# Layer 2's inputs issued behind the attention's last sum, image 2 loaded into score tiles, and scan carries copied by POOL

## The chip, the cores and the metric

The kernel runs on one core of one Trainium2 chip. The metric is device time in microseconds. The engines are PE (TensorE, matmuls), DVE (VectorE), ACT (ScalarE), POOL (GpSimd) and SP (SyncE, which here only issues DMAs); each works through its own queue in order.

## The reference

The input x is 4 images of 512 channels by 32x32 positions, in float32. Two layers follow one another, each added to its input.

```
x = x + mamba(groupnorm(x))
x = x + pab(groupnorm(x))
```

The first layer, per image: layer norm over channels, a projection to 2 x 1024 rows (xm and z), a causal convolution of 4 taps and SiLU (xs), a projection of xs to dt, B and C, and then for each of 1024 rows and 16 states a recurrence over the 1024 positions:

```
h = exp(dt*A) * h + (dt*xs) * B        # one scan for each row and state
y = sum over states of h * C
out = ((y + xs*D) * silu(z)) @ W_out
```

The second layer, per image: two 1x1 convolutions to 64 channels (top, center), their product of all positions with all positions (1024x1024 scores), a softmax over the whole map, the product of that map with a 3x3 convolution of the image, the image added, and a second 3x3 convolution.

## The kernel before, in words

**First layer.** The work is cut into stages: image b, pair of 128-row groups e (0 to 3), half h of the 1024 positions. That makes 4 x 4 x 2 = 32 stages of 16 states s each; one stage and state is a `unit`. In a unit, ACT makes the decay exp(dt*A) (L832). The input part comes in one of two ways: for nine states, ACT scales transposed rows by B (L844) and PE transposes them back (L870); for the other seven, POOL multiplies by B (L859). DVE runs two scans of 128x512 (L884), one for each 128-row group j. The product with C follows: for states 1, 5, 9 and 13 (`C_ON_DVE`) on DVE (L900, in two halves), for the other twelve on POOL (L906, one instruction of 128x1024). PE adds the result into y (L913). A stage ends when ACT copies y out (L936).

The second half of the positions goes on where the first ended. So for h = 0, DVE copies the last column of each scan to `carry_sb` right behind the scan (L889, 128x1), and the scan with h = 1 of the same state, one stage later, starts from it.

The order of all this isn't written out. Each operation is a `step` with an engine, a cost in us, its reads and writes and a priority. A planner (`Plan.issue`) runs through these costs, always takes the step that can start first or is most urgent, and so writes the order of every engine's queue. A scan costs 1.18 in it, 1.32 with the copy; the C product on POOL 2.31. Other work is laid between the units by priority: the projection and convolution of the next image, the output projection of the image before, and the transform of 3x3 weights for the second layer ("fill" steps on POOL).

**Second layer.** The 3x3 convolutions are done in a transformed domain (Winograd, 4 x 2 outputs). `conv3` takes an image, makes its transformed inputs in three pairs (for the first pair `first_inputs`: ACT L1393, POOL L1394, DVE L1396 and L1397, then `spread` L1374 to L1377; for the other pairs POOL L1456, L1457, L1466, L1467 and DVE L1460, L1469), and multiplies them with 24 weight tiles of 1 MB, loaded by SP into three buffers (L1490, L1494). DVE combines the products (L1510). Five PSUM buffers (`pm`) hold these products; three others (`ps`) serve everything else.

Per image b the order in the program is: `conv3("b")`, then `attend` (PE L1546 multiplies the score tiles with the convolution's result in 8 blocks; DVE adds each block into the image, L1559), and in between `scores` for the next image of the pair (PE L1324 makes top and center, ACT copies them to SBUF at L1329 and L1336; PE L1345 makes the scores, ACT copies them into eight `st` tiles at L1349; DVE takes maxima, L1350). During the attention of images 0 and 1, DVE also transforms the second convolution's remaining weights (`piece`, L1421 to L1432). After both images of a pair, `conv3("o")` runs for each, and `finish` adds the result to the stored input and writes it out (SP loads at L1576, PE L1586, DVE L1591, ACT stores at L1601).

`norm` makes the normalised image: ACT issues 8 loads of 256 KB (L1285) into a tile with the tag "v", which the transformed inputs use too, DVE takes statistics (L1292, L1293), PE averages over groups (L1299, L1303), ACT makes the root, DVE writes the image (L1306). For image 2 this happens inside `conv3("o1")`, through `mid`. Here the framework's scheduler sets the order on each engine, from the program's order and its own view of what is ready; tiles of one tag take turns in that tag's buffers, and an instruction waits for the buffer's last users.

Of the kernel before, what the change touches and what calls it, by code (L numbers as in the profile page):

```python
# [8 lines left out]
F32 = mybir.dt.float32  # L9
# [6 lines left out]
P = 128  # L16
B, C, HH, WW = 4, 512, 32, 32
L = HH * WW
NCC = C // P
# [4 lines left out]
T = 512  # L24
# [145 lines left out]
def mamba_then_pab_kernel(  # L170
# [25 lines left out]
    nc = tc.nc  # L196
# [23 lines left out]
    brow = []  # L220
# [46 lines left out]
    image = {}  # L267
# [6 lines left out]
    with ExitStack() as l0:  # L274
# [539 lines left out]
        def unit(b, e, h, s, y):  # L814
# [49 lines left out]
            for j, u in enumerate(us):  # L864
                part = parts[j]
                if on_act:

                    def turn(j=j, u=u):
                        for k in range(NK):
                            nc.tensor.transpose(  # L870
                                u()[:, k * P : (k + 1) * P], sc()[:, k, j, :], ident
                            )

                    step(
                        "ACT", EXP, lambda j=j: decay(j, hc()[:, j]), [dt], [part], prio, "exp",
                        holds=[hc],
                    )
                    step("PE", 4 * TR, turn, [sc], [u], prio - PRM["kt"])
                else:
                    step("ACT", EXP, lambda j=j, u=u: decay(j, u()), [dt], [u], prio - PRM["ke"], "exp")  # L880

                def scan(j=j, u=u):
                    ht = u() if on_dve else hc()[:, j]
                    nc.vector.tensor_tensor_scan(  # L884
                        ht, *((hc()[:, j], u()) if on_act else (u(), hc()[:, j])),
                        carry_sb[:, j, s : s + 1] if h else 0.0, ALU.mult, ALU.add,
                    )
                    if h == 0:
                        nc.vector.tensor_copy(carry_sb[:, j, s : s + 1], ht[:, T - 1 : T])  # L889

                before, behind = ([carry[s][j]], []) if h else ([], [carry[s][j]])
                step(
                    "DVE", SCAN if h else SCAN + 0.14, scan,
                    [part if on_act else hc, u, *before],
                    [u if on_dve else part, *behind], prio - 1, holds=[hc],
                )
                if on_dve:
                    step(
                        "DVE", 0.6,
                        lambda j=j, u=u: nc.vector.tensor_mul(hc()[:, j], u(), c_bc()[:, 0]),  # L900
                        [u, c_bc], [part], prio, holds=[hc],
                    )
            if not on_dve:
                step(
                    "POOL", 2.31,
                    lambda: nc.gpsimd.tensor_mul(hc(), hc(), c_bc().to_broadcast([P, 2, T])),  # L906
                    [c_bc], parts, prio, holds=[hc],
                )
            for j in range(2):

# [349 lines left out]
    with ExitStack() as l1:  # L1260
# [15 lines left out]
        NMC = L // P  # L1276
        HR = T // WW

        def norm(b):

            xg = padded(b, *((cpool, "image"), (gp, "xg"))[b % 2])
            t = xp.tile([P, NCC, L], F32, tag="v", name=f"x1t_{b}")
            for c in range(NCC):
                for h in range(NH):
                    nc.scalar.dma_start(  # L1285
                        t[:, c, h * T : (h + 1) * T], x1[b][h][c * P : (c + 1) * P, :]
                    )
            mv = spool.tile([P, NCC, 2], F32, tag="mv", name=f"mv_l1_{b}")
            for c in range(NCC):
                bs = spool.tile([P, NH, 6], F32, tag="bs", name=f"bs_l1_{b}_{c}")  # L1290
                for h in range(NH):
                    nc.vector.bn_stats(bs[:, h, :], t[:, c, h * T : (h + 1) * T])  # L1292
                nc.vector.bn_aggr(mv[:, c, :], bs)  # L1293
            mean, rstd, dev = (
                spool.tile([P, NCC], F32, tag=n, name=f"{n}_l1_{b}")
                for n in ("gmean", "grstd", "gdev")
            )
            p1 = ps.tile([P, T], F32, tag="ps", name=f"pm_l1_{b}")
            nc.tensor.matmul(p1[:, :NCC], gm_sb, mv[:, :, 0], start=True, stop=True)  # L1299
# [5 lines left out]
            for c in range(NCC):  # L1305
                nc.vector.tensor_scalar(  # L1306
                    xg[:, c, 1 : HH + 1, 1 : WW + 1],
                    t[:, c].rearrange("p (h w) -> p h w", w=WW),
                    mean[:, c : c + 1], rstd[:, c : c + 1], ALU.subtract, ALU.mult,
                )  # L1310
            image[b] = xg

        def scores(b, xg):

# [121 lines left out]
            for q in (1, 2):  # L1436
                nc.sync.dma_start(dst[q], o[:, q - 1])

        def conv3(name, xg, u, bias, first=None, late=None, mid=None):

# [34 lines left out]
            y = [None] * 4  # L1475
            for pair in PAIRS:
                if pair == (1, 2):
                    v = first or first_inputs(name, xg)
                    if mid:
                        mid()  # L1480
                else:
                    v = spread(name, pair[0], inputs(pair))
                ns = []
# [53 lines left out]
        def attend(b, xg, st, rp, xb, between, also):  # L1537

            ahead = piece_taps(also[0]) if also else None


            for k in range(NCC * NH):
                j, h = divmod(k, NH)
                pt = ps.tile([P, C], F32, tag="ps", name=f"pat_{b}_{j}_{h}")
                for m in range(NMC):
                    nc.tensor.matmul(  # L1546
                        pt, st[m][:, 2 * P * j + h : 2 * P * (j + 1) : 2],
                        xb[m // 2][:, m % 2, :],
                        start=(m == 0), stop=(m == NMC - 1),
                    )  # L1550
# [8 lines left out]
                nc.vector.scalar_tensor_tensor(  # L1559
                    img, pt.rearrange("p (h w) -> p h w", w=WW), rz, img,  # L1560
                    ALU.mult, ALU.add,
                )
                if also:
                    taps = piece_taps(also[k + 1]) if k + 1 < len(also) else None
                    piece(*ahead)
                    ahead = taps
                    if taps is None:
                        also = []

        dst = [out[b].rearrange("(c p) h w -> p c (h w)", p=P) for b in range(B)]  # L1570

# [44 lines left out]
        def normed(b):  # L1616
            for _ in norm(b):
                pass

        left = list(range(EARLY, NPC))  # L1620
        half = len(left) // 2
        st, rp = scores(0, image[0])
        for a in range(0, B, 2):
            for b in (a, a + 1):
                xb = conv3(f"b{b}", image[b], ub, brow[0])
                also = left[b * half : (b + 1) * half] if not a else []
                after, v = iter(()), None
                if b == a:
                    after = norm(b + 1)
                    next(after)  # L1630
                else:
                    v = first_inputs(f"o{a}", image[a])
                attend(b, image[b], st, rp, xb, after, also)
                if b == a:
                    st, rp = scores(b + 1, image[b + 1])
            finish(a, conv3(f"o{a}", image[a], uo, brow[1], v))
            if a + 2 == B:
                last(a + 1, image[a + 1], None)
                break
            y = conv3(f"o{a + 1}", image[a + 1], uo, brow[1], mid=lambda: normed(a + 2))  # L1640
            finish(a + 1, y)
            st, rp = scores(a + 2, image[a + 2])


# [55 lines left out]
```

## Time and profile before

| | us |
|---|---|
| runs: median of 3 | 3060.0 |
| runs: lowest and highest | 3053.99, 3060.22 |
| the profiled execution's own time | 3048.93 |
| its span in the profile | 3047.1 |

| engine | busy us | share of the span |
|---|---|---|
| PE | 2742.4 | 90% |
| DVE | 2402.3 | 79% |
| POOL | 2022.1 | 66% |
| ACT | 1842.4 | 60% |

The two layers differ: from 187 to 1992 us (31 of the 32 stages) DVE is busy for 1689.9 of 1805 us, PE for 1606.1, ACT for 1595.6 and POOL for 1562.9; after that PE is the busy one. In lines of the profile, a name such as `da` or `uw_b` is a tile's name without its number: `hc` of the source is `da` (states with B on ACT) or `dbx` (the others). `[5.86 <-DVE xg L1559]` says that the engine stood idle for 5.86 us before the line's first instruction, and that this wait ended with DVE's instruction of line 1559. A float32 matmul shows as two passes. A PE busy time can hold slow passes: the granted clock of a stretch tells.

### The profile page before, as it was taken

The page shows a single profiled execution, that of the slowest core. Times are in us where ns is not written, and L with a number is a line of the kernel's source. Part 1 is how long each engine was busy: PE and PEld are TensorE (multiplying, and loading weights), DVE is VectorE, ACT ScalarE, POOL GpSimd, SP SyncE. Part 2 cuts the span into 40 slices and gives each one's busy share as a digit, 9 for nine tenths or more (in the row PEclk, how much of TensorE's full clock was granted, in tenths as well). Part 3 has the DMA queues.
Part 4 walks back from the last instruction along what each step waited for, and adds up shares of the span by engine and source line. Part 5 has one row for each costly group of instructions (what it writes and reads, how often), then busy time and mean ns, then how long its engine had stood idle before and what let it go on. Part 6 is the DMA issues. An engine that isn't in the chain of part 4 may idle for free.

```text
span 3047.1 us, 35912 instructions
## 1 busy us (share of the span) xinstructions
PE 2742.4 (90%) x11512; PEld 1607.5 (53%) x11512; DVE 2402.3 (79%) x3171; ACT 1842.4 (60%) x3179; POOL 2022.1 (66%) x1047
## 2 busy tenths in 40 slices
PE   4789789999889999889999978799899999999998
PEld 2346556656666666556666655544344444444444
DVE  3469999989999989989999999976857575456164
ACT  4579989998789999789999888731110013030000
POOL 7899977899967889967889999843321331323132
PEclk8899999999999999989999999999999999999999
DMA  6766534567734567734566654748588896727497
GB/s 179 213 192 210 168 121 141 164 207 231 232 109 145 166 180 229 251 116 133 168 184 213 209 177 141 171 154 297 170 286 263 301 330 246 264 70 275 138 316 256
DMA packets 408947, 610.47 MB, mean 200 GB/s; under 512 B 46488, under 2 KB 245400, under 8 KB 384184
## 3 DMA queue, kind: packets, MB, share of 16 engines
q1 hardware_dynamic: 399952, 593.67, 61.8%
q10 hardware_dynamic: 8648, 14.26, 1.3%
q8 instruction: 92, 1.51, 0.2%
q14 instruction: 95, 0.78, 0.1%
q0 software_dynamic: 160, 0.26, 0.0%
HBM read 511.09 MB, written 96.99 MB: 200 GB/s over the span
## 4 chain that ended last, share of the span: by engine, by line
PE 45%; DVE 23%; ACT 16%; DMA 6%; issue 5%; POOL 4%; SPq 1%; ACTq 0%; DVEq 0%; POOLq 0%
PE m_o L1494 10%; PE m_b L1494 9%; DVE da L884 7%; PE y L913 5%; PE pz L394 4%; ACT sc L844 4%; PE pat L1546 4%; DVE u L884 3%; ACT da L832 3%; PE po L394 2%; PE u L870 2%; ACT u L832 2%; DVE dbx L884 2%; PE pxm L394 2%; PE psc L1345 2%
## 5 line engine op out<-in xcount | busy, mean ns | idle before, releaser
L906 POOL TENSOR_TENSOR da<-da,cbc 128x1024 f32<-128x1024 f32 x288 | 680.3, 2367 | 151.3 <-DVE carry_sb L889 63.6
L859 POOL TENSOR_TENSOR dbx<-dtx,bbc 128x1024 f32<-128x1024 f32 x224 | 529.6, 2368 | 59.1 <-PE y L913 34.9
L844 ACT ACTIVATE sc<-dtxt,bt_sb 128x256 f32<-128x256 f32 x1152 | 504.6, 497 | 46.2 <-PE u L870 46.0
L832 ACT ACTIVATE da<-dt,a_sb 128x512 f32<-128x512 f32 x576 | 395.0, 713 | 39.2 <-PE y L913 33.5
L884 DVE TENSOR_TENSOR_SCAN da<-da,carry_sb,u 128x512 f32<-128x512 f32 x288 | 356.0, 1262 | 27.3 <-PE u L870 22.0
L913 PE MATMUL y<-ident,da 128*128 128x128 f32 x2304 | 320.4, 283 | 58.3 <-POOL da L906 54.4
L870 PE MATMUL u<-ident,sc 128*128 128x128 f32 x2304 | 336.1, 278 | 35.3 <-DVE da L884 24.9
L913 PEld LDWEIGHTS y<-ident,da 128*128 128x128 f32 x2304 | 268.5, 145 | 161.2 <-POOL da L906 109.9
L884 DVE TENSOR_TENSOR_SCAN da<-da,u 128x512 f32<-128x512 f32 x288 | 348.8, 1211 | 3.9 <-PE u L870 3.6
L1494 PE MATMUL m_o<-uw_o,v_o 128*128 128x512 f32 x768 | 337.9, 599 | 4.4 <-DMA uw_o<-u_o 4.4
L1494 PE MATMUL m_b<-uw_b,v_b 128*128 128x512 f32 x768 | 333.4, 593 | 4.1 <-DMA uw_b<-u_b 4.1
L870 PEld LDWEIGHTS u<-ident,sc 128*128 128x128 f32 x2304 | 268.4, 143 | 112.2 <-DVE da L884 37.2
L832 ACT ACTIVATE u<-dt,a_sb 128x512 f32<-128x512 f32 x448 | 297.4, 681 | 36.8 <-DVE dbx L900 14.0
L394 PE MATMUL pxm<-xt,winc 128*128 128x345 f32 (+3 forms) x704 | 251.3, 499 | 29.3 <-DMA winc<-in_w_in_dram 16.5
L913 PE MATMUL y<-ident,dbx 128*128 128x128 f32 x1792 | 252.9, 279 | 23.7 <-POOL dbx L906 14.4
L913 PEld LDWEIGHTS y<-ident,dbx 128*128 128x128 f32 x1792 | 207.5, 143 | 99.7 <-issue 32.2
L394 PE MATMUL pz<-xt,winc 128*128 128x512 f32 x512 | 242.1, 600 | 11.7 <-ACT sz L707 2.1
L1494 PEld LDWEIGHTS m_o<-uw_o,v_o 128*128 128x128 f32 x768 | 145.9, 192 | 188.0 <-issue 180.7
L1494 PEld LDWEIGHTS m_b<-uw_b,v_b 128*128 128x128 f32 x768 | 145.0, 190 | 188.9 <-issue 179.5
L906 POOL TENSOR_TENSOR dbx<-dbx,cbc 128x1024 f32<-128x1024 f32 x96 | 226.7, 2362 | 26.0 <-DVE carry_sb L889 17.5
L1546 PE MATMUL pat<-y_b,st 128*128 128x512 f32 x512 | 221.6, 593 | 1.6 <-DVE rz L1555 1.5
L394 PEld LDWEIGHTS pxm<-xt,winc 128*128 128x128 f32 x704 | 132.0, 198 | 117.1 <-issue 62.1
(235 smaller groups left out, 4331.5 us busy)
## 6 DMA issues: line engine op xcount, KB each, us to landing
cbc<-bcd SPq DMA_DIRECT2D x512, 256.0 KB, 3.6
uw_b<-u_b SPq DMA_DIRECT2D x96, 1024.0 KB, 4.8
uw_o<-u_o SPq DMA_DIRECT2D x96, 1024.0 KB, 4.8
bbc<-bcd SPq DMA_DIRECT2D x224, 256.0 KB, 3.6
u_b<-work SPq DMA_DIRECT2D x192, 128.0 KB, 2.8
winc<-in_w_in_dram SPq DMA_DIRECT2D x72, 256.0 KB, 3.8
szd<-sz SPq DMA_DIRECT2D x32, 512.0 KB, 3.5
szl<-szd SPq DMA_DIRECT2D x32, 512.0 KB, 5.0
```

What stands on the lines that cost most here:

```text
L394: lambda k=k, lhs=lhs, rhs=rhs: nc.tensor.matmul(p()[:, at : at + cols], lhs(), rhs(), start=(k == 0), stop=(k == n - 1)),
L832: nc.scalar.activation(t, dt()[:, j], AF.Exp, scale=a_sb[:, at : at + 1])
L844: nc.scalar.activation(sc()[:, k], dtxt()[:, k], AF.Copy, scale=bt[:, at, s : s + 1])
L859: lambda: nc.gpsimd.tensor_mul(hc(), dtx(), b_bc().to_broadcast([P, 2, T])),
L870: nc.tensor.transpose(u()[:, k * P : (k + 1) * P], sc()[:, k, j, :], ident)
L884: nc.vector.tensor_tensor_scan(ht, *((hc()[:, j], u()) if on_act else (u(), hc()[:, j])), carry_sb[:, j, s : s + 1] if h else 0.0, ALU.mul ...
L906: lambda: nc.gpsimd.tensor_mul(hc(), hc(), c_bc().to_broadcast([P, 2, T])),
L913: nc.tensor.matmul(y[j]()[:, k, :], hc()[:, j, k * P : (k + 1) * P], ident, start=(s == 0 and k == 0), stop=(s == NS - 1 and k == NK - 1), ...
L1345: nc.tensor.matmul(pt, top[:, m * P : (m + 1) * P], center[:, h * T : (h + 1) * T], start=True, stop=True,)
L1494: nc.tensor.matmul(m[q], v[:, q, k, c, :], w[:, c, :], start=(c == 0), stop=(c == NCC - 1 and not extra),)
L1546: nc.tensor.matmul(pt, st[m][:, 2 * P * j + h : 2 * P * (j + 1) : 2], xb[m // 2][:, m % 2, :], start=(m == 0), stop=(m == NMC - 1),)
```

## The change

In the scans, for the twelve states with the C product on POOL, DVE no longer copies the carries; POOL copies both last columns of a unit (128x2) right ahead of its C product. The planner's costs follow (scan 1.18; POOL 2.5 for the two), and `carry` is now written by the POOL step. In the second layer, `attend` returns its last sum, and the inputs of the second image of a pair (`first_inputs`, all engines' instructions; the one on DVE gets the edge) are issued behind it on DVE. `norm` is cut in three parts. For image 2 its data goes into four tiles of tag "st", its loads and statistics come ahead of `conv3("o0")`, the mean behind it, and the root and the image behind `finish` of image 0.

```diff
-                    if h == 0:
+                    if h == 0 and on_dve:
                         nc.vector.tensor_copy(carry_sb[:, j, s : s + 1], ht[:, T - 1 : T])
 
-                before, behind = ([carry[s][j]], []) if h else ([], [carry[s][j]])
-                step(
-                    "DVE", SCAN if h else SCAN + 0.14, scan,
+                before, behind = ([carry[s][j]], []) if h else ([], [carry[s][j]] if on_dve else [])
+                step(
+                    "DVE", SCAN + 0.14 if h == 0 and on_dve else SCAN, scan,
...
             if not on_dve:
-                step(
-                    "POOL", 2.31,
-                    lambda: nc.gpsimd.tensor_mul(hc(), hc(), c_bc().to_broadcast([P, 2, T])),
-                    [c_bc], parts, prio, holds=[hc],
+                def times_c():
+                    if h == 0:
+                        nc.gpsimd.tensor_copy(carry_sb[:, :, s : s + 1], hc()[:, :, T - 1 : T])
+                    nc.gpsimd.tensor_mul(hc(), hc(), c_bc().to_broadcast([P, 2, T]))
+
+                step(
+                    "POOL", 2.31 if h else 2.5, times_c,
+                    [c_bc], [*parts, *([] if h else carry[s])], prio, holds=[hc],
                 )
...
-        def norm(b):
-
-            xg = padded(b, *((cpool, "image"), (gp, "xg"))[b % 2])
-            t = xp.tile([P, NCC, L], F32, tag="v", name=f"x1t_{b}")
+        def norm(b, spare=False):
+
+            if spare:
+                ts = [xp.tile([P, L], F32, tag="st", name=f"x1t_{b}_{c}", bufs=NMC) for c in range(NCC)]
+            else:
+                t = xp.tile([P, NCC, L], F32, tag="v", name=f"x1t_{b}")
+                ts = [t[:, c] for c in range(NCC)]
...
+            yield
             p1 = ps.tile([P, T], F32, tag="ps", name=f"pm_l1_{b}")
             nc.tensor.matmul(p1[:, :NCC], gm_sb, mv[:, :, 0], start=True, stop=True)
             deviation(p1, mv, mean, dev)
...
-            for c in range(NCC):
+            xg = image[b] = padded(b, *((cpool, "image"), (gp, "xg"))[b % 2])
+            for c, t in enumerate(ts):
...
-                    v = first or first_inputs(name, xg)
-                    if mid:
-                        mid()
+                    with tc.issue_after(behind.ins) if behind else ExitStack():
+                        v = first or first_inputs(name, xg)
...
-                nc.vector.scalar_tensor_tensor(
+                ins = nc.vector.scalar_tensor_tensor(
                     img, pt.rearrange("p (h w) -> p h w", w=WW), rz, img,
                     ALU.mult, ALU.add,
                 )
...
+            return ins
...
         for a in range(0, B, 2):
+            ins = None
             for b in (a, a + 1):
-                xb = conv3(f"b{b}", image[b], ub, brow[0])
+                xb = conv3(f"b{b}", image[b], ub, brow[0], behind=ins)
...
                 if b == a:
                     after = norm(b + 1)
                     next(after)
+                    next(after)
                 else:
                     v = first_inputs(f"o{a}", image[a])
-                attend(b, image[b], st, rp, xb, after, also)
+                ins = attend(b, image[b], st, rp, xb, after, also)
...
-            finish(a, conv3(f"o{a}", image[a], uo, brow[1], v))
+            if a + 2 < B:
+                after = norm(a + 2, True)
+                next(after)
+            y = conv3(f"o{a}", image[a], uo, brow[1], v)
+            next(after, None)
+            finish(a, y)
...
-            y = conv3(f"o{a + 1}", image[a + 1], uo, brow[1], mid=lambda: normed(a + 2))
-            finish(a + 1, y)
+            next(after, None)
+            finish(a + 1, conv3(f"o{a + 1}", image[a + 1], uo, brow[1]))
```

More of the change, by code (lines that the diff above doesn't have):

```diff
@@ L1277, in mamba_then_pab_kernel @@
         HR = T // WW
-        def norm(b):
-            xg = padded(b, *((cpool, "image"), (gp, "xg"))[b % 2])
-            t = xp.tile([P, NCC, L], F32, tag="v", name=f"x1t_{b}")
-            for c in range(NCC):
+        def norm(b, spare=False):
[5 more added lines that the diff above has]
+            for c, t in enumerate(ts):
                 for h in range(NH):
                     nc.scalar.dma_start(
-                        t[:, c, h * T : (h + 1) * T], x1[b][h][c * P : (c + 1) * P, :]
+                        t[:, h * T : (h + 1) * T], x1[b][h][c * P : (c + 1) * P, :]
                     )
             mv = spool.tile([P, NCC, 2], F32, tag="mv", name=f"mv_l1_{b}")
-            for c in range(NCC):
+            for c, t in enumerate(ts):
                 bs = spool.tile([P, NH, 6], F32, tag="bs", name=f"bs_l1_{b}_{c}")
                 for h in range(NH):
-                    nc.vector.bn_stats(bs[:, h, :], t[:, c, h * T : (h + 1) * T])
+                    nc.vector.bn_stats(bs[:, h, :], t[:, h * T : (h + 1) * T])
                 nc.vector.bn_aggr(mv[:, c, :], bs)
@@ L1304, in norm @@
             rsqrt(rstd, p2[:, :NCC])
-            for c in range(NCC):
+            xg = image[b] = padded(b, *((cpool, "image"), (gp, "xg"))[b % 2])
+            for c, t in enumerate(ts):
                 nc.vector.tensor_scalar(
                     xg[:, c, 1 : HH + 1, 1 : WW + 1],
-                    t[:, c].rearrange("p (h w) -> p h w", w=WW),
+                    t.rearrange("p (h w) -> p h w", w=WW),
                     mean[:, c : c + 1], rstd[:, c : c + 1], ALU.subtract, ALU.mult,
                 )
-            image[b] = xg
         def scores(b, xg):
@@ L1437, in piece, with conv3 @@
                 nc.sync.dma_start(dst[q], o[:, q - 1])
-        def conv3(name, xg, u, bias, first=None, late=None, mid=None):
+        def conv3(name, xg, u, bias, first=None, late=None, behind=None):
             def rows(a):
@@ L1614, in last @@
                 (nc.scalar, nc.sync)[j % 2].dma_start(dst[b][:, j, :], o[j])
-        def normed(b):
-            for _ in norm(b):
-                pass
         left = list(range(EARLY, NPC))
```

## The prediction

> **What bounds the kernel now.** I read the engines' busy shares by stage first, since the two parts of the change sit in different layers. Layer 1 (the scans) runs to about 1995 us, layer 2 from there to 3047. A stretch of undisturbed scan stages of the last image (columns: stretch, length, then busy us of PE, PE weight load, DVE, ACT, POOL):
>
> ```profile
> 1643.00:1944.00 301.00, 259.67 (x1527) 182.60 (x1525) 295.41 (x383) 252.16 (x465) 282.20 (x132) 0.99 0.61 178
> ```
> and all that DVE waits for in it:
> ```profile
> DVE dbx L884 <- ACT u L832: 0.9, 1, 0.9
> DVE da L884 <- PE u L870: 0.6, 1, 0.6
> DVE dbx L884 <- POOL dbx L859: 0.3, 1, 0.3
> ```
> DVE waits 1.8 of 301 us: it sets the pace here, with POOL (282) close behind. A second sign: taking a stage to end at its y copies (L936), the stages of image 3 with h = 0 (which save carries) last 50.5, 51.3, 52.5, 51.0 us, those with h = 1 50.1, 48.6, 47.9, 48.4. The cost of a carry copy, from DVE in order of time:
> ```profile
> 1000.28 1.22 DVE L884 TENSOR_TENSOR_SCAN u<-u,dbx 128x512 f32<-128x512 f32 x1
> 1001.53 0.16 DVE L889 COPY carry_sb<-u 128x1 f32<-128x1 f32 x1
> 1001.61 1.22 DVE L884 TENSOR_TENSOR_SCAN u<-u,dbx 128x512 f32<-128x512 f32 x1
> ```
> Scan to scan takes 1.33 us with a copy; without one, two scans in a row take 2.37, so 1.19 each. A copy costs DVE 0.14 us, though it is booked as 0.15.
>
> In layer 2 the chain of waits is nearly all PE, so I looked for PE's gaps. Two large ones touch the change. The first stands between image 0's attention and image 1's scores:
> ```profile
> 2170.91 3.61 PE L1324 MATMUL pt<-xg,wt_sb 128*128 128x512 f32 x8
> 2176.76 3.71 PE L1324 MATMUL pt<-xg,wt_sb 128*128 128x512 f32 x8 [2.24 <-DVE xg L1559]
> 2180.31 1.88 PE L1494 MATMUL m_b<-uw_b,v_b 128*128 128x512 f32 x4
> 2188.05 5.36 PE L1345 MATMUL psc<-center,top 128*128 128x512 f32 x6 [5.86 <-DVE xg L1559]
> 2198.03 14.08 PE L1345 MATMUL psc<-center,top 128*128 128x512 f32 x26 [4.62 <-ACT st L1349]
> ```
> DVE and ACT show why: the last two sums (L1559) stand among image 1's transform inputs, and the score copies stand behind an input of the output convolution that waits for DVE.
> ```profile
> 2175.96 0.75 DVE L1559 SCALAR_TENSOR_TENSOR xg<-pat,rz,xg 128x512 f32<-128x512 f32 x1
> 2182.55 3.55 DVE L1376 TENSOR_TENSOR v_b<-rr_b 128x1024 f32<-128x1024 f32 x1
> 2187.16 0.74 DVE L1559 SCALAR_TENSOR_TENSOR xg<-pat,rz,xg 128x512 f32<-128x512 f32 x1
> 2196.39 1.11 ACT L1393 ACTIVATE e_o<-xg 128x1088 f32<-128x1088 f32 x1 [13.94 <-DVE rr_b L1469]
> ```
> The second gap is in the output convolution of image 1, where PE's group mean for image 2 waits for statistics queued on DVE behind an output sum:
> ```profile
> 2456.59 1.41 DVE L1591 TENSOR_TENSOR o<-o,po 128x256 f32<-128x256 f32 x4 [6.66 <-DMA o<-x]
> 2460.72 0.56 PE L1299 MATMUL pm_l<-mv_l,gm_sb 128*128 128x4 f32 x2 [6.05 <-DVE mv_l L1293]
> 2461.14 5.35 PE L1494 MATMUL m_o<-uw_o,v_o 128*128 128x512 f32 x6
> ```
> And a smaller one, where image 2's loads will now go:
> ```profile
> 2353.83 8.70 PE L1494 MATMUL m_o<-uw_o,v_o 128*128 128x512 f32 x16 [3.05 <-DMA uw_o<-u_o]
> ```
>
> **What the Trainium skill says.** "TensorE: Matmul & The Clock Gate", What's actually happening: after an idle window of about 3.4 us the array falls to half clock and needs a busy window to come back. The trace agrees: granted clock 0.50 at 2188 to 2190 and at 2462 to 2466, 0.86 us a pass in place of 0.43; even the 3.05 us gap costs clock, the 2.24 us gap doesn't. "GPSIMD Engine Reference", 3.1 Elementwise: GpSimd reaches an instruction over two software hops, against DVE's dispatch of some 156 ns; no figure for a tiny copy. The trace gives a fixed part: 0.73, 1.28 and 2.37 us for 256, 512 and 1024 elements leave 0.185 us at none. The same page, 1. Specifications: GpSimd shares SBUF interfaces with DVE instructions of two SBUF inputs. Agrees: L1375 and L1376 took 3.55 us each beside POOL's L1466 and L1467, 1.22 elsewhere. "DMA: Bandwidth & Descriptors", Queues, rings and completion order: each DMA engine takes turns between queues. The trace can't show the turns, but x1t loads land in a median 7.2 us and the four times larger weights in 4.8.
>
> **Part 1, scans.** 12 of 16 states multiply by C on POOL. For h = 0 that is 4 images x 4 pairs x 12 = 192 units, and 384 DVE copies go: 384 x 0.14 = 53.8 us off DVE, 3.4 in each of the 16 stages with h = 0. Added are 192 POOL copies of 128x2. No such row exists. From below, the 128x1 memset: 0.10 us; from above, the fixed 0.185 plus a semaphore's wait, 0.25. I take 0.15 (two POOL products follow one another 0.06 closer than their length, so 0.185 is partly covered): 1.8 us a stage, 29 us in all, between 19 and 48. The y matmuls behind each product see the scan end 0.14 sooner and POOL 0.15 later: even. The h = 1 scan that reads the carry comes 16 units later, so that wait is hidden.
>
> Now who takes over. In an undisturbed stage POOL has 19 products at 2.31 us and two at 1.28: 46.4. With the copies 48.2, where the stage lasts 51.3 and DVE falls from 51 to 47.6. So POOL is next; I count 2.5 us for each of the three such stages of image 3 (7.5), and 2 for the two of images 1 and 2 (4). In the six heavy h = 0 stages, which carry the next image's projection (62 to 73 us; DVE 91 to 97% busy, POOL 63 to 92%, ACT 85 to 98%), 2 each: 12. First stages of an image are ACT's (50.9 of 51 us at 1592 to 1643): 0.5 each, 1.5; image 0's early ones 1. Sum 26. The planner's new costs move every later step; the built kernel shows 7 more ACT table loads in layer 1 at 1.28 us = 9 us, five in image 1, of which I put 4 on the path. **Layer 1: -22 us**, bounds -45 (nearly all of the 53.8) and +5 (POOL and ACT eat it).
>
> **Part 2, inputs behind the last sum.** In the built order both sums precede L1396, and the score copies precede e_o. From 2170.91 to the end of the scores PE has 16 + 4 + 32 = 52 passes at 0.43 = 22.4 us but takes until 2211.95, 41.0: 12.7 idle, 5.9 half clock. Afterwards: sums at 2173.5 and 2174.2 (L1432 ends at 2173.5), so the second pt starts at once and ends at 2177.9. The first transform group needs L1374; L1396 (free of the rr buffer at 2174.75) starts at 2174.9, L1374 ends at 2178.6, so PE waits 0.7. ACT's top copies end at 2180.0, the scores start at 2180.4 and, copied in 0.58 us each against PE's 0.86, end at 2194.1. **-17.9 us** (-12 if an input or the weights hold PE again; -18.6 at most). What is late next: DVE mixes eight maxima (1.22) with the remaining inputs and reaches L1510 near 2206.5; PE needs the accumulator that it frees at about 2215. Next weights again wait for SP's o loads, which wait for the scores: the 1.3 us gap at 2223 stays. For image 3 PE had no gap; inputs are ready at 2706.6 and PE needs them at 2709.0. Nothing, but only 2.4 us of cover.
>
> **Part 3, image 2 in score tiles.** Its 8 loads (2 MB), statistics (8 x 0.68 + 4 x 0.19 = 6.2 us of DVE) move from 2439 to about 2348, when attention frees the tiles. At 2460 the wait goes: 6.05 + (5.35 - 2.6) = 8.8 us; the two tiny matmuls remain (0.5), and the weights, which follow the o load on SP, should land just in time. **-8 us** (-5 to -8.5). The price: at 2348 PE is already waiting for the first uw_o. Sharing turns with x1t it lands some 2.5 us later, and the longer idle costs about 0.9 of clock: **+3.4 us** (0 to 6). ACT's issues hold up e_o1 and f_o1, and DVE's statistics the last sum and L1510; the next PE user of either (the sixth accumulator, near 2377) is over 10 us away. The four border memsets (1.2 us of POOL) move to where POOL idles.
>
> **Sum.** -22 - 17.9 - 8 + 3.4 = -44.5. The profiled execution took 3048.9 us (span 3047.1), so 3004.4. The runs shown have a median of 3060.0, 11.1 above; on that footing 3015.5, and I give 3016.
>
> **Rivals.** POOL takes DVE's place in layer 1 (22%): for it, 46.4 of 51 us and POOL's 13.7 us of idle in the stretch above; against, its room in heavy stages. Layer 1 gives about 2, total 3036. DVE really was the only limit (15%): for it, the 1.8 us of waits; layer 1 gives 40, total 2998. The layer 2 gap only changes its releaser (8%), for instance weights or inputs hold the scores: part 2 gives 4, total 3030. Slower (6%): the tiny POOL copy is dear. Each h = 0 stage then ends with POOL at 46.4 + 12c; layer 2's 22.5 is lost over 16 stages from 46.4 + 12c - 51.3 = 1.4, c = 0.53 us; at 0.8 us the stages lose 4.7 each, 75 in all, total 3112. Against it: the 0.185. That the edits don't act is excluded for the order (the build shows it).
>
> **Numbers.** Forecast case 45% (its own range 3006 to 3026), rivals 22, 15, 8 and 6%, and 4% for a re-planned layer 1 that gives the gain back. Within 0.2% (6 us, what can be told from no change here): 4%; slower 6%; faster 90%. The range 2994 to 3042 leaves out the slow cases and the far end of the quick ones.
>
> **What would show it.** Right: stages with h = 0 about as long as those with h = 1; POOL copies of 0.1 to 0.25 us; scores of image 1 in one run of 14 us with no idle before; no wait at L1299 for image 2; a longer wait for uw_o near 2350. Wrong: DVE idle in the stages of image 3 with POOL at 98%, copies over 0.5 us, or PE waiting for uw_b or v_b before the scores.

## The result, and the profile after

| | before | after |
|---|---|---|
| runs: median, us | 3056.99 (4 runs) | 3012.82 (4 runs) |
| runs: lowest and highest | 3049.64, 3060.22 | 3012.06, 3018.19 |
| the profiled execution's own time, its span | 3048.93, 3047.1 | 3013.52, 3011.5 |
| busy us of PE, DVE, ACT, POOL | 2742.4, 2402.3, 1842.4, 2022.1 | 2732.6, 2324.8, 1846.0, 2054.5 |

The ratio is 0.9872, with a 95% interval of 0.9851 to 0.9893: 44 us between the medians, 35.4 between the two profiled executions. The forecast was 3016.

Where the 35.6 us of span went can be read off marks that both traces have. Image 0's first scores in layer 2 start at 2014.4 before and at 2000.4 after, so 14.0 lie ahead of them, in the scans, and 21.6 behind. In layer 2 the largest single piece is image 1's score gap, from PE's first `pt` to the end of the scores: 41.0 us before (2170.91 to 2211.95), 22.3 after (2158.74 to 2181.08), so 18.7.

**Scans.** An undisturbed stretch of the last image after the change (stretch, length, then busy us of PE, PE weight load, DVE, ACT, POOL):

```profile
1630.00:1930.00 300.00, 265.41 (x1562) 188.56 (x1560) 287.44 (x314) 255.96 (x473) 289.78 (x164) 0.97 0.58 179
```

What DVE waits for in it (total, times, longest):

```profile
DVE res L1001 <- PE po L394: 7.5, 6, 4.4
DVE dbx L884 <- ACT u L832: 2.4, 3, 1.3
DVE da L884 <- PE u L870: 1.6, 2, 1.0
DVE total L1061 <- PE po L394: 1.2, 1, 1.2
...
```

DVE fell from 295.4 of 301 us to 287.4 of 300, and POOL rose from 282.2 to 289.8: POOL is now slightly the busier of the two, and DVE waits 13.9 us in all where it waited 1.8. The new instruction, in order of time on POOL:

```profile
1684.72 0.18 POOL L906 COPY carry_sb<-da 128x2 f32<-128x2 f32 x1
1684.98 2.37 POOL L907 TENSOR_TENSOR da<-da,cbc 128x1024 f32<-128x1024 f32 x1
1687.30 2.38 POOL L859 TENSOR_TENSOR dbx<-dtx,bbc 128x1024 f32<-128x1024 f32 x1
1689.62 0.19 POOL L906 COPY carry_sb<-da 128x2 f32<-128x2 f32 x1
1689.89 2.37 POOL L907 TENSOR_TENSOR da<-da,cbc 128x1024 f32<-128x1024 f32 x1
```

The copy itself is 0.18 or 0.19 us, but the product that follows starts 0.26 to 0.27 after the copy's start. From the start of one long instruction to that of the next POOL needs 2.32 us without a copy between them (1684.98 to 1687.30) and 2.59 with one (1687.30 to 1689.89). Over all such pairs without idle time the medians are 2.32 and 2.58. So a copy costs POOL 0.25 to 0.27 us.

**Layer 2, the score gap.** PE's order of time after (the bracket is idle time before, and what ended it):

```profile
2158.74 7.05 PE L1332 MATMUL pt<-xg,wt_sb 128*128 128x512 f32 x16
2165.64 1.88 PE L1501 MATMUL m_b<-uw_b,v_b 128*128 128x512 f32 x4
2167.35 13.90 PE L1353 MATMUL psc<-center,top 128*128 128x512 f32 x32
2181.08 5.31 PE L1501 MATMUL m_b<-uw_b,v_b 128*128 128x512 f32 x12
2213.23 3.27 PE L1501 MATMUL m_b<-uw_b,v_b 128*128 128x512 f32 x7 [1.55 <-ACT e_b L1509]
```

And DVE's, at the place where the sums and the inputs used to be mixed:

```profile
2159.47 1.40 DVE L1566 SCALAR_TENSOR_TENSOR xg<-pat,rz,xg 128x512 f32<-128x512 f32 x2
2160.80 1.29 DVE L1404 TENSOR_TENSOR rr_b<-e_b,f_b 128x1088 f32<-128x1088 f32 x1
```

Both sums (L1566, formerly L1559) go ahead of the first input, the two `pt` follow one another, and the scores are one run of 13.9 us. The three waits of 2.24, 5.86 and 4.62 us are gone. A new one of 1.55 us comes later.

**Layer 2, the second convolutions.** PE's first weights of image 0's output convolution, and image 2's group mean with what follows it:

```profile
2325.19 8.53 PE L1501 MATMUL m_o<-uw_o,v_o 128*128 128x512 f32 x16 [5.04 <-DMA uw_o<-u_o]
...
2410.34 0.28 PE L1307 MATMUL pm_l<-mv_l,gm_sb 128*128 128x4 f32 x2
...
2426.72 3.70 PE L1501 MATMUL m_o<-uw_o,v_o 128*128 128x512 f32 x8 [0.20 <-DMA uw_o<-u_o]
```

The 6.05 us wait of the group mean (L1299 before, L1307 now) is gone. The wait for the first `uw_o` grew from 3.05 to 5.04.

### The profile page after: what moved, and what is told of

It reads as the page before. It is cut to its first block, busy times and chain, and to the rows that moved or that the text cites. A ratio compares the mean times of both kernels' runs of the same rounds, so it can differ in the third digit from the quotient of the medians.

```text
span 3011.5 us, 35733 instructions
## 1 busy us (share of the span) xinstructions
PE 2732.6 (91%) x11512; PEld 1611.4 (54%) x11512; DVE 2324.8 (77%) x2787; ACT 1846.0 (61%) x3186; POOL 2054.5 (68%) x1239
## 4 chain that ended last, share of the span: by engine, by line
PE 39%; ACT 14%; DVE 14%; POOL 6%; issue 5%; DMA 4%; SPq 0%; DVEq 0%; POOLq 0%; ACTq 0%
PE m_o L1501 11%; PE m_b L1501 8%; PE pat L1553 4%; PE y L917 4%; ACT sc L844 3%; DVE da L884 3%; PE po L394 3%; POOL da L907 3%; PE pz L394 2%; ACT da L832 2%; ACT u L832 2%; PE u L870 2%; DVE u L884 2%; DVE dbx L884 2%; PE pp L730 1%
## 5 line engine op out<-in xcount | busy, mean ns | idle before, releaser
L859 POOL TENSOR_TENSOR dbx<-dtx,bbc 128x1024 f32<-128x1024 f32 x224 | 529.5, 2371 | 35.7 <-PE y L917 18.7
L870 PE MATMUL u<-ident,sc 128*128 128x128 f32 x2304 | 329.3, 279 | 35.1 <-DVE da L884 26.6
L884 DVE TENSOR_TENSOR_SCAN da<-da,u 128x512 f32<-128x512 f32 x288 | 338.4, 1202 | 18.6 <-PE u L870 16.7
```

The costliest lines, as they stand in the source:

```text
L859: lambda: nc.gpsimd.tensor_mul(hc(), dtx(), b_bc().to_broadcast([P, 2, T])),
L870: nc.tensor.transpose(u()[:, k * P : (k + 1) * P], sc()[:, k, j, :], ident)
L884: nc.vector.tensor_tensor_scan(ht, *((hc()[:, j], u()) if on_act else (u(), hc()[:, j])), carry_sb[:, j, s : s + 1] if h else 0.0, ALU.mul ...
```

## The experiments

Ratios are against runs of the kernel before on the same chip. For the scans I also use one length from each profile: from the first stage's first y copy to the last stage's first y copy ("scan length"). It repeats well between executions with the same scans: 1754.5, 1756.7 and 1756.0 us for the scans of before (the kernel before, e1, e5), 1738.7, 1738.2, 1739.3 and 1737.8 for those of after (after, e2, e8, e12).

**One part alone.** e1 has the scans of before with all of after's layer 2, e2 the reverse; e5 is before with the issue-behind edge alone.

```diff
 e1: carry copies and costs as before; layer 2 as after
 e2: carry copies and costs as after; layer 2 as before
 e5: before, and
+                    with tc.issue_after(behind.ins) if behind else ExitStack():
+                        v = first or first_inputs(name, xg)
```

> Only the changes of the second layer; the scans are those of before, with DVE copying the carries. My theory: from the traces of before and after, the second layer gives 21 us (18.7 at the scores of image 1, 7 at the output convolution of image 1, less 2 at the first output weights and about 3 of smaller waits elsewhere), so about 0.993 of before, 3035 us. Rival: the whole gain is the second layer's and re-ordered scans gave nothing: 0.987. Rival: the layers are not additive, since the scans' new end moves what the second layer meets: below 12 us.

> Only the changes of the scans; the second layer is that of before. My theory: the first scores of image 0 start 14 us sooner, as in the traces, and nothing follows: about 0.9955, 3043 us. Rival: layer 1 gives the 22 us that I forecast and the profiled execution of before was a fast one: 0.993.

> The kernel before with one edit: the second image's inputs of a pair are issued behind the attention's last sum. My theory: this alone closes the gap at the scores of image 1, 18 us, and pays back 2 to 3 us at two later waits for ACT's copy of an accumulator: 15 us faster, ratio 0.995. Rival: without the norm of image 2 moved, DVE and SP are late elsewhere and eat it: under 8 us.

| | median us | ratio | 95% |
|---|---|---|---|
| e1, layer 2 alone | 3033.23 | 0.9945 | 0.9933 to 0.9957 |
| e2, scans alone | 3032.61 | 0.9941 | 0.9930 to 0.9953 |
| e5, edge alone | 3037.91 | 0.9945 | 0.9928 to 0.9962 |

In us that is -17 for layer 2, -18 for the scans: together -35 of the change's -39 (1.28% of 3050). The parts add up within the intervals. The edge alone gives as much as all of layer 2, so image 2's new place nets nothing that runs can resolve. The profiles show why. From image 1's `pz` (the small matmul early in the attention that adds up the softmax's row sums) to the first bias pass of image 0's output convolution takes 60.1 us before, 61.95 after. Single profiles scatter here, so I take all that are kept: 58.2 to 60.7 us in the five with before's layer 2 or with the edge alone (before, e2, e3, e5, e10), 61.95 to 63.7 in the six with after's layer 2 (after, e1, e4, e7, e9, e11). The means differ by 3.6: that is what the early loads cost. From there to image 2's first scores takes 192.5 before, 185.5 after, 185.4 in e1: 7.0 gained.

**The moved copy without the new plan.** e3 has POOL's copies but gives the planner the costs of before, so each queue keeps its old order.

```diff
-                    "DVE", SCAN + 0.14 if h == 0 and on_dve else SCAN, scan,
+                    "DVE", SCAN + 0.14 if h == 0 else SCAN, scan,
...
-                    "POOL", 2.31 if h else 2.5, times_c,
+                    "POOL", 2.31, times_c,
 (layer 2 as before)
```

> The scans' change with the planner's costs left as before (scan 1.32 with h = 0, C product 2.31), so that every queue keeps the order of before and only the 384 copies on DVE give way to 192 on POOL. My theory: the copy costs POOL 0.27 us (0.19 and 0.08 until the product starts), POOL takes over the pace in stages without a projection, and the gain is about the same as with the new order: 10 to 16 us. Rival: the new order with its 7 more table loads cost some 8 us, then this one gains 20 to 24 us. Other rival: the gain came from the new order, then this one gains under 5 us.

Measured: 3061.29, ratio 1.0041 (1.0029 to 1.0053), 12.5 us slower than before, where my theory and both rivals had it faster. The same instructions on the same engines, in the old order, lose time. DVE's waits over 187 to 1992 us, of before and then of e3 (total, times, longest):

```profile
DVE da L884 <- PE u L870: 25.6, 20, 2.7
DVE dbx L884 <- ACT u L832: 14.1, 13, 2.9
```
```profile
DVE da L884 <- PE u L870: 42.7, 36, 3.8
DVE dbx L884 <- ACT u L832: 26.5, 25, 3.1
```

DVE has less to do, 1617 us in place of 1690, and waits more. But these waits alone don't explain the loss. In e10 (below; its line numbers are one higher), which has the same order and no copies of the twelve states at all, more than half of their rise is there too:

```profile
DVE da L885 <- PE u L871: 35.3, 28, 3.8
DVE dbx L885 <- ACT u L833: 22.3, 20, 3.1
```

And yet e10 is faster than before. What sets e3 apart from e10 is POOL's copies alone. PE's waits for POOL's C products, ahead of the y matmuls, add up to 68.8 us before, 74.4 in e10 and 91.0 in e3. That these waits rose is measured; which of them sets the pace was not separated.

**The new plan without the moved copy, and no copy at all.** e9 keeps after's queue orders but leaves the copies on DVE. e4 is after without POOL's copies, e10 has before's scan order without the copies of the twelve states and before's layer 2.

```diff
 e9 (costs of after; layer 2 as after)
-                    if h == 0 and on_dve:
+                    if h == 0:
                         nc.vector.tensor_copy(carry_sb[:, j, s : s + 1], ht[:, T - 1 : T])
...
-                    if h == 0:
-                        nc.gpsimd.tensor_copy(carry_sb[:, :, s : s + 1], hc()[:, :, T - 1 : T])
 e4 (after), e10 (order of before): no copy for these states,
+        nc.gpsimd.memset(carry_sb, 0.0)
```

> The changed kernel with the order of all queues kept, but the carries copied by DVE behind each scan, as before. Theory one: the new order helps only because it fits the new durations, so with DVE's 54 us back the scans lose all of the gain and more, 17 to 30 us above the changed kernel. Theory two: the new order is simply a better one, whichever engine copies: within 5 us of the changed kernel. Theory three: the work on DVE decides, then 10 to 15 us above it.

> The changed kernel, same order of all queues, with POOL's 192 carry copies left out: for the twelve states whose C product is POOL's, the carry stays at zero, so the second half of the positions starts from an empty state there. My theory: POOL's copies set the pace in 16 stages, 12 x 0.27 = 3.2 us a stage, and about a third to a half of these 51 us is on the path: 15 to 25 us below the changed kernel, near 2993 us. Rival: POOL's copies fall into its waits and cost nothing: same as the changed kernel within 4 us.

> The kernel before, same order of all queues, with DVE's 384 carry copies left out and none on POOL: the carry of the twelve states with POOL's C product stays at zero, so their second half starts from an empty state. Theory one: with the queues' order fixed, the 54 us that DVE gains turn into waits; under 10 us faster, ratio above 0.997, so the loss of the run with POOL copies in the old order (+12.5 us) is POOL's copies standing in the fixed order. Theory two: DVE sets the pace, 25 us or more faster, below 0.992.

| | median us | ratio | 95% |
|---|---|---|---|
| e9, new order, DVE copies | 3037.73 | 0.9950 | 0.9931 to 0.9968 |
| e4, new order, no copies | 3005.15 | 0.9852 | 0.9839 to 0.9864 |
| e10, old order, no copies | 3037.72 | 0.9950 | 0.9932 to 0.9968 |

With layer 2's -17 taken off e9 and e4, the scans alone stand as follows against before (runs), with the scan length from the profile in brackets:

| scans, us | old order | new order |
|---|---|---|
| DVE copies | 0 (1754.5) | about +2 (1759.4) |
| no copies | -15 (1741.5) | about -28 (1729.0) |
| POOL copies | +12.5 (1763.6) | -18 (1738.7) |

Each figure from runs has an interval of some 4 to 6 us either way, and the two measures agree cell by cell to a few us. With the copies made at all, the gain needs both halves: the new order with the old copies is worth nothing, the old order with the new copies loses. In the old order the POOL copies cost 22 us of scan length over no copies, in the new one 10; that is less than the 15 to 25 that I expected of e4. e9 is 24 us above after by the ratios, as its theory one had it. e10 lies between its two theories: of the 54 us taken off DVE, 15 reach the total.

**Is the order lucky, and how dear is a copy?** e11 charges the planner 2.58 for copy and product, the measured 2.31 + 0.27, in place of 2.5. e7 makes each POOL copy twice in after's order.

```diff
 e11
-                    "POOL", 2.31 if h else 2.5, times_c,
+                    "POOL", 2.31 if h else 2.58, times_c,
 e7
+                        for _ in range(2):
-                        nc.gpsimd.tensor_copy(carry_sb[:, :, s : s + 1], hc()[:, :, T - 1 : T])
+                            nc.gpsimd.tensor_copy(carry_sb[:, :, s : s + 1], hc()[:, :, T - 1 : T])
```

> The changed kernel with one number changed: the planner charges POOL 2.58 us for copy and product in place of 2.5, as the trace has it (0.27 for the copy). My theory: a closer charge gives an order that fits at least as well, within 6 us of the changed kernel on either side. Rival: the order that the change got was a lucky one, and any other costs 10 us or more.

> The changed kernel, same order of all queues, with each of POOL's 192 carry copies done twice. Leaving them out saved 8 us of the 51 that they take. My theory: POOL has little room left in the stages that it now paces, so a second copy costs more than the first, 15 to 30 us above the changed kernel. Rival: the first copy's price holds, 8 us more, since POOL's waits still take most of it.

e11: 3015.01, ratio 0.9871 (0.9852 to 0.9889), the same as after, though it reshuffles the stages (image 0 takes 7.1 us longer, image 2 3.7 less). So the gain doesn't hang on this one order. e7: 3043.97, ratio 0.9980 (0.9973 to 0.9987), 33 us above after by the ratios. POOL in e7:

```profile
1707.53 0.45 POOL L907 COPY carry_sb<-da 128x2 f32<-128x2 f32 x2
1708.06 2.36 POOL L908 TENSOR_TENSOR da<-da,cbc 128x1024 f32<-128x1024 f32 x1
```

Two copies hold the product up by 0.53 us, and lengthen the distance between POOL's instructions from 2.32 to 2.83, so by 0.50. The scan lengths are 1729.0, 1738.7 and 1768.3 for none, one and two: the first costs 9.7, the second 29.6. Each copy is 49 to 51 us of POOL in all (192 x 0.25 to 0.265). Of the first a fifth is on the path, of the second well over half.

**The new waits of layer 2.** In e8 image 2's loads are issued behind ACT's first accumulator copy of the output convolution. In e12 the later inputs of the second image are issued behind the scores' maxima as well.

```diff
 e8
-                    nc.scalar.activation(e, m[2], AF.Copy, scale=al / 2)
+                    act = nc.scalar.activation(e, m[2], AF.Copy, scale=al / 2)
+                    if mid and p == 1:
+                        with tc.issue_after(act.ins):
+                            mid()
 e12: e8, and
-                        v = spread(name, pair[0], inputs(pair))
+                        with tc.issue_after(rest.ins) if rest else ExitStack():
+                            v = spread(name, pair[0], inputs(pair))
```

> The changed kernel with image 2's eight loads issued behind ACT's first accumulator copy of the first output convolution, so that three weight tiles go ahead of them. My theory: the loads share the DMA engines with the first output weights and cost 2 to 5 us there (5.0 us of wait and half clock); that wait returns to about 2.8 us and no other grows by as much: 2 to 4 us faster than the changed kernel. Rival: the loads collide with the next weights just as hard, nothing gained.

> The late loads, and the later transform inputs of the second image of a pair issued behind the scores' maxima on DVE. My theory: PE's waits for ACT's accumulator copy (1.55 us for image 1, 0.93 for image 3) come from the maxima standing between the inputs, which puts the exponentials and with them that copy late; both go: 4 to 6 us faster than the changed kernel. Rival: the inputs of the second pair are then late themselves and PE waits for v_b: no gain over the late loads alone.

e8: 3014.15, ratio 0.9879 (0.9864 to 0.9894), not told apart from after. PE's first `uw_o` in e8:

```profile
2321.68 8.82 PE L1501 MATMUL m_o<-uw_o,v_o 128*128 128x512 f32 x16 [2.88 <-DMA uw_o<-u_o]
```

The wait is back from 5.04 to 2.88, so the loads did make it longer, and the stretch from image 1's `pz` is back at 60.1. Image 2's later start then gives 0.5 back (186.0 for 185.5). That leaves 1.4 us against after's own profile, and some 2.5 against the mean of the six; too little for the runs.

e12: 3008.15, ratio 0.9864 (0.9849 to 0.9879), 6 us under e8 by the medians, but not told apart from e8 or from after by the intervals. Why DVE's maxima matter is seen in after, on POOL and then on ACT:

```profile
2202.87 0.38 POOL L1363 PARTITION_ALL_REDUCE ma<-mp  x1 [6.90 <-issue]
```
```profile
2189.03 1.11 ACT L1401 ACTIVATE e_o<-xg 128x1088 f32<-128x1088 f32 x1 [7.16 <-DVE rr_b L1477]
...
2203.53 1.15 ACT L1367 ACTIVATE st<-st,ma 128x1024 f32<-128x1024 f32 x1 [11.90 <-DVE ma L1364]
...
2212.60 1.06 ACT L1509 ACTIVATE e_b<-m_b 128x512 f32<-128x512 f32 x2
```

The maxima stand between transform inputs on DVE; the last ends at 2190.1, the common maximum comes at 2203.3, and the eight exponentials keep ACT until 2212.6. Only then does ACT copy the accumulators that PE needs: its wait of 1.55 us. Of the way from the last maximum to the common one, most is POOL's. Its reduction over the partitions (L1363) stands behind two transform inputs of the output convolution, which end at 2195.97, and then starts 6.90 us later without anything in the profile that it waits for. For image 3, in after:

```profile
2719.81 20.44 PE L1501 MATMUL m_b<-uw_b,v_b 128*128 128x512 f32 x47 [0.93 <-ACT e_b L1509]
```

In e12 the maxima are done by 2183.5. POOL has nothing just ahead of its reduction there, which starts 0.14 us after its input is ready, so the common maximum comes at 2186.2: 7 us are won on DVE, and 10 more on POOL. PE's products run on:

```profile
2181.45 5.31 PE L1502 MATMUL m_b<-uw_b,v_b 128*128 128x512 f32 x12
...
2187.74 28.59 PE L1502 MATMUL m_b<-uw_b,v_b 128*128 128x512 f32 x66
```

From the first scores to `pz` image 1 takes 102.5 us in place of 104.35, image 3 102.5 in place of 103.7.

**A split.** e13 is e12 with DVE keeping the copies of six of the twelve states, in the first two pairs of each image and in all of image 3.

```diff
+            keep = h == 0 and (on_dve or ((b == B - 1 or e < 2) and s in (2, 4, 7, 10, 12, 15)))
+            moved = h == 0 and not keep
...
-                    if h == 0 and on_dve:
+                    if keep:
...
-                    "POOL", 2.31 if h else 2.5, times_c,
+                    "POOL", 2.58 if moved else 2.31, times_c,
```

> As the run before, and the carry copies divided: in the stages of pairs 0 and 1 and of image 3, where POOL has no room, DVE keeps six of the twelve copies; elsewhere POOL has all; POOL charged 2.58. My theory: a pair of undisturbed stages asks 96.0 us of POOL and 93.5 of DVE with all copies on POOL; with half 94.4 and 95.2, so 3 to 8 us faster than the run before. Rival: the new plan's own luck, up to 10 us either way, hides it.

Measured: 3005.58, ratio 0.9853 (0.9839 to 0.9866): the lowest median of the versions that compute everything, some 6 us under after by the ratios. Its interval overlaps those of e12 and of after, so it isn't told apart from either. Its scan length is 1736.4 against 1737.8 in e12, but the images moved more than their sum: image 2 takes 8.0 us less than in e12 (469.5 for 477.5), image 3 5.4 more (399.6 for 394.2). So giving half of the copies back to DVE seems to help in image 2 and to hurt in image 3; as the whole plan changed with them, that isn't shown.

## Why the prediction was right, step by step

**Part 1, -22 forecast.** The runs give -18 (e2). The profiles give 15 to 19 us by scan length, 14.0 by image 0's first scores against the profiled execution of before, and 20 against those of e1 and e5, which have the same scans and start these scores at 2020.4 and 2020.6. So the profile of before that the sum was made against was itself some 6 us quick. The direction was right, and so was who comes next, POOL. That DVE set the pace was right in part: e10 takes 54 us off DVE, puts nothing on POOL, and gains 15. Two terms were mis-sized.

The first is "I take 0.15". It measures 0.25 to 0.27, at the upper of the bounds 0.10 and 0.25: 49 to 51 us of POOL, not 29. The 54 us that DVE lost were thus nearly all given to POOL. It cost 10 us of the path (e4 against after in scan length; 0.2% in the ratios); the rest went into time in which POOL had waited.

The second is the 2 us a stage in images 1 and 2. By image, the scans took 413.3, 469.4, 471.6 and 400.3 us before, and 402.9, 463.3, 478.3 and 394.3 after: image 2 didn't gain, it lost 6.7. Here is an h = 0 stage of image 2 before, then the same one after (columns as above):

```profile
1223.00:1275.00 52.00, 50.52 (x268) 34.97 (x269) 47.49 (x73) 39.89 (x75) 51.33 (x31) 0.97 0.74 241
```
```profile
1209.20:1264.50 55.30, 51.99 (x274) 34.51 (x275) 44.38 (x52) 40.53 (x76) 53.87 (x42) 1.00 0.73 236
```

POOL was full already, 51.3 of 52 us, since here it also makes weight transforms, so its copies lengthen the stage: by its y copies this one takes 53.9 us with none (e4), 55.4 with one a unit (after) and 58.5 with two (e7), all in the same order. For stages like this one I had taken over the 46.4 us of POOL work of the last image, where no such transforms are. Image 2 as a whole takes 472.4 without copies in the new order (e4), 478.3 with them; 470.6 without in the old order (e10), 477.7 with them (e3).

The stages of image 3 show the rest: with h = 0 they last 51.2, 49.8, 50.3 and 52.1 us, where 50.5, 51.3, 52.5 and 51.0 were; my 2.5 for each of three came to about 1.5, 2.2 and a loss of 1.1. What I called the sign of being right, "stages with h = 0 about as long as those with h = 1", didn't come: h = 1 stages got shorter too (50.2, 48.8, 44.9, 47.0). The gain is one of the whole plan, not of the stages that lose a copy.

What the sum didn't have at all is the size of the planner's part. "The planner's new costs move every later step" stood there only as a cost of 4 us. By the table above the plan is worth 25 to 30 us once the copies have moved: from +9 in the old order to -16 in the new by scan length, from +12.5 to -18 by the runs. A sum of what each engine has to do can't tell these two orders apart: for the order of before it would have forecast a gain as well, and e3 lost. That it came within 4 us of the runs is in part luck.

One reading of the profile was loose: the 13.7 us given for POOL's idle time in the stretch before leave out, above all, 4.6 us without a named releaser. In all POOL was idle for 18.8 of the 301.

**Part 2, -17.9 forecast.** Measured -18.7 in the gap, and -17 in runs (e5). The step from 52 passes x 0.43 = 22.4 us was right; the 0.7 us wait for the first inputs isn't in after's profile, but the six others with the edge and without the slow passes told of below have 0.5 to 1.0 us there, for inputs or weights. "The 1.3 us gap at 2223 stays" failed: PE doesn't wait for weights there, but for 1.55 us for ACT, behind the exponentials. I had followed DVE's queue past the mixed maxima to L1510, and not the chain from the maxima through POOL's reduction and the exponentials to ACT's accumulator copy. The same for image 3: "Nothing" measured 1.2 us between its `pz` and image 2's (0.93 of it the wait shown). e12 shows that the mixed order of DVE is behind both: with the maxima first, both waits are gone.

**Part 3, -8 and +3.4 forecast.** Measured -7.0, and +1.8 by the profiles of before and after, +3.6 over all profiles. Both halves of the price came as forecast. The wait for the first `uw_o` has a median of 2.85 us in the five profiles without early loads and of 5.0 in the six with them: 2.2 longer, 2.5 forecast. And the longer wait costs clock. The 16 passes behind it take 8.67 us in the median without early loads and 9.7 with them: 1.0 more, 0.9 forecast. After's own profile, with 8.53, is the quickest of its six and hides this. Two others, e5 without early loads and e1 with them, show it more fully:

```profile
2343.97 7.13 PE L1495 MATMUL m_o<-uw_o,v_o 128*128 128x512 f32 x16 [2.80 <-DMA uw_o<-u_o]
```
```profile
2347.57 9.75 PE L1497 MATMUL m_o<-uw_o,v_o 128*128 128x512 f32 x16 [5.55 <-DMA uw_o<-u_o]
```

The net forecast was a gain of 4.6; the profiles give 3.4 in the mean, which the runs of e1 and e5 can't tell from nothing.

**The sum.** Span against span the forecast was -44.5, measured -35.6: 8 short in the scans, and some 1 us short in layer 2, where two further things stood against the -18.7. One was predicted nowhere: image 0's attention from `pz` to PE's `pt` ran 1.7 us longer, in slow passes. The 112 passes there take 50.04 us behind a wait of 1.54 us after, and 48.34 behind one of 1.53 before. Four of the fourteen profiles have this (after, e1, e7, e11). e9, with the same layer 2 and the same wait, doesn't, so its cause is open. The other is the 1.2 of image 3. That the median nevertheless came out within 4 us of the forecast is luck: the 9 us missing in the span were made up by the 11.1 us that I had put between profile and median, while after's median lies within 1 us of its profile.

**The rivals.** "POOL takes DVE's place" (22%) had the engine right and the size wrong: POOL did, and the scans still gained 16 to 18. "DVE really was the only limit" (15%) is close to e4, with nothing put on POOL: -28 of its -40. The slower rival put the point where layer 2's gain is eaten at c = 0.53 us. e7 comes close to that c, with 0.50 to 0.53 for its two copies: the scans of e7 are 12 to 14 us longer than before's, and the total is still 0.2% under before. So the mechanism is real, and the point where nothing is left lies a little higher. What the list lacked is the case of e3, a slower kernel with a cheap copy and an old plan.

**Left open.** Which of the longer waits in e3 sets the pace, and why image 0's attention had slow passes in some profiles and not in others.

## What to carry to other kernels

When an instruction moves from the engine that sets the pace to the next busiest, look at every stage of the receiver, not at one clean stretch: where it is already full, the move lengthens the stage. And count the order of the queues as part of the edit: here the same move lost 12.5 us in the old order and won 18 in the order planned for it. Don't read a cost of one or two us from one profile of each kernel: here the price of the early loads was 1.8 us by one pair of profiles and 3.6 over eleven. For a tiny instruction count how much later the next one starts, not its duration.

## What the runs showed of the hardware

- A POOL copy of 128x2 lasts 189 ns in the median (178 to 259), and the product behind it starts 0.27 us after the copy's start in the median; with two copies it is 0.53 (the lines of e7). From one of POOL's 128x1024 instructions to the next it is 2.32 us with no copy between, 2.58 with one and 2.83 with two. So a copy costs about 0.25, more than its own row shows. DVE's 128x1 copy is the other way round: booked 0.16, it holds up the next scan by 0.14.
- 2 MB of image loads issued ahead of the first weight tile lengthened PE's wait for that tile from 3.05 to 5.04 us; with the loads issued later (e8) it was 2.88.
- The 16 passes behind this wait took 7.13 us after waits of 2.55, 2.66 and 2.80 us (e12, e3, e5), 8.67 to 8.83 after the five waits of 2.85 to 3.47, and 8.53 to 10.21 after the six of 4.77 to 5.55. The length of a wait doesn't decide alone: in image 0's attention, waits of 1.53 to 1.57 us were followed by slow passes in after, e1 and e11, and by none in before, e5 and e9.
- POOL's reduction over the partitions started 6.90 us after the end of POOL's instruction before it in after, and 5.70 in e5, with nothing named that it waited for. In e12, where POOL had been idle for 13.6 us, it started 0.14 us after its input.
